# A macaron layer on one core: VectorE's stream steps beside the first FFN go behind the product of each FFN step, and the streams get more steps between engines

## The chip, the core and the metric

One core of one Trainium2 chip runs the whole layer in one launch. A core has five engines that work side by side, each through its own queue in order: TensorE (PE, with its weight loads as PEld), VectorE (DVE), ScalarE (ACT), GpSimd (POOL), and SyncE (SP), which here only starts DMA transfers. They wait for each other through semaphores. The metric is the device time of the core in microseconds, lower is better; for the kernel before it is the median of three runs.

## The reference

The layer takes x of shape (4, 1024, 128): 4096 tokens of width 128. It adds half of a routed FFN, then an attention block, then half of the same FFN again. Cut to what matters:

```python
x = x + 0.5 * ffn(layernorm(x))      # 8 experts, all computed; weights by a router
x = x + attn(layernorm(x))           # 16 heads of 64, low-rank q/k/v through 64 latents, rope
x = x + 0.5 * ffn(layernorm(x))

def ffn(x):
    inh = sigmoid(x @ Wr / temperature)
    in_zone = (inh >= LOWER) & (inh <= 0.5)
    w = exp(-|inh - 1/e| / 0.1) * in_zone
    fb = exp(-|inh - 1/e| / 0.3), kept for its two largest of 8, normed to sum 1
    w = where(sum(w) < 1e-8, fb, w);  w = w / max(sum(w), 1e-8)
    h = silu(x @ Wg[e]) * (x @ Wu[e])          # for each expert e
    return sum over e of w[e] * (h @ Wd[e])

def attn(x):                          # its result already holds x as the residual
    h = layernorm(x) * ln_scale + ln_bias
    cq, ckv = h @ w_down_q.T, h @ w_down_kv.T
    q, k = rope(cq @ w_up_q.T), rope(ckv @ w_up_k.T);  v = ckv @ w_up_v.T
    return softmax(q @ k.T / 8) @ v @ w_out.T + x
```

## The kernel before

**Main loops.** The tokens lie in X, in SBUF, as eight blocks of 512. The program has three stretches. The first FFN (`ffn`) runs 64 steps n, eight blocks by eight experts. A step is six matmuls of 512 columns (L411: gate and up, each in three parts), Silu on ScalarE (L413), the product of Silu and up on VectorE (L419, the "product"), and four matmuls down (L382) for a step three earlier; then a gather adds the result, weighted by the router, to X: by VectorE (L390) for a few experts, else by ScalarE into `dtmp` (L394) and POOL (L395). Gate and up of step n take two of three PSUM banks in turn, so that the gate of step n+2 writes the bank that the product of step n has read: if a product is late, TensorE waits two steps on. The attention runs 128 groups g of four slots: scores (L723), exponentials (L727), running sums on POOL (L739), values (L746), maxima for a later group (L697, L698), and every other group the denominators (`den`, L758) and the output (L779, L790). The second FFN (`ffn2`) runs 64 steps again (L490, L493, L503, L504, L498, L445).

**Streams.** What prepares later work is written as Python generators, which the loops advance a step at a time, so that their instructions are interleaved by hand in each engine's queue. `ffn_pre` prepares two blocks for an FFN: statistics on VectorE (`stats`, L216 and L219), inverse root on POOL (`power`, L223 to L226), norm on ScalarE (`norm`, L235), transposes on PE (L264), a split into two parts on VectorE (L266, L267), router matmuls (L277, L278), then `route`, some ten short VectorE steps with a few of ScalarE and POOL. `attn_pre` prepares a batch for attention: the same twice over, then latents (L555, L561, L562) that go to DRAM (the store at L564) and come back for `rope`. `rope` makes rotated q and k of 512 tokens (matmuls L605, four VectorE products L592, POOL L613, L615, L624, ScalarE L620, two stores to DRAM). In a generator, work k of the first half-block and work k minus a lag of the second are emitted in the same step, so the numbers k set the distance between an instruction and what needs it.

**Who advances them.** Beside the first FFN, `bg1` is called at four points of a step: before gate and up, before down, before the product, behind the product. It gives each stream credit (`bg`): stream 0 (`ffn_pre`) RATE1/4 = 0.6 steps a point, stream 2 (weights, `attn_pre(0)`, nine ropes) RATE2/4 = 0.575. In the attention `step` is called three times a group and takes what the stream's next kind allows (OTHER, VECTOR or PE); VECTOR steps are taken in every group while `hurry` holds (g below 16 or in the last 24), else in even groups. Beside the second FFN `bg2` advances the last `ffn_pre` one step an FFN step from n = 17, two from n = 22. All transposes and small matmuls of the streams beside the first FFN use one PSUM bank (`aux`), so each waits until the one before has been read.

Of the kernel before, what the change touches and what calls it, by code (L numbers as in the profile page):

```python
# [13 lines left out]
ALU = mybir.AluOpType  # L14
# [20 lines left out]
NROPE = 9  # L35
ACTS = (4, 6, 7)
WLAG, GS, GD = 4, 17, 22
RATE0, RATE1, RATE2, RATE3 = 1.55, 2.4, 2.3, 1.4


class Kernel:
# [176 lines left out]
            for i in range(4):  # L218
                nc.vector.bn_aggr(mv[:, i, :], st[:, i, :])  # L219

    def power(self, mv, rstd):
        nc = self.nc
        nc.gpsimd.tensor_scalar(rstd[:, :, 1], mv[:, :, 1], EPS, None, ALU.add)  # L223
        nc.gpsimd.tensor_tensor(rstd[:, :, 0], rstd[:, :, 1], self.neghalf[:, :4], ALU.pow)
        nc.gpsimd.tensor_tensor(rstd[:, :, 1], mv[:, :, 0], rstd[:, :, 0], ALU.mult)
        nc.gpsimd.tensor_scalar(rstd[:, :, 1], rstd[:, :, 1], -1.0, None, ALU.mult)  # L226

    def norm(self, out, src, mv, rstd, half, vector=False):

# [8 lines left out]
    def ffn_pre(self, P, blks, xs, w_out, done=None, rows=None):  # L238
        nc = self.nc
        X = self.X  # L240
        n = len(blks)
        mv = P.tile([128, TPB, 2], F32, name="mvf")
        rstd = P.tile([128, TPB, 2], F32, name="rstdf")
        z = P.tile([128, TPB, E], F32, name="z")
        st = {}

        def stage(k, h, blk):
            t0 = 4 * blk
            hs = slice(4 * h, 4 * h + 4)
            src = [X[:, t0 + i, :] for i in range(4)]  # L250
            if k == 0:
                st["st", h] = self.small.tile([128, 4, 6], F32, name="st")
            if k in (0, 1):
                self.stats(st["st", h], src, mv[:, hs], k)
            elif k == 3:
                self.power(mv[:, hs], rstd[:, hs])
            elif k in (5, 6):
                if k == 5:
                    st["y", h] = P.tile([128, 4, 128], F32, name="yf", tag="f0")
                self.norm(st["y", h], src, mv[:, hs], rstd[:, hs], k - 5, blk == 0 and done is None)  # L260
            elif k == 8:
                ps = self.aux()
                for i in range(4):
                    nc.tensor.transpose(ps[:, i * 128:(i + 1) * 128], st["y", h][:, i, :], self.ident)  # L264
                x2 = st["x", h] = xs(blk)
                nc.vector.tensor_copy(x2[:, 0, :], ps)  # L266
                nc.vector.tensor_tensor(x2[:, 1, :], ps, self.f(x2[:, 0, :]), ALU.subtract)  # L267
                self.ready.add(blk)
            elif k == 12:
                x2 = st["x", h]  # L270
                if done:
                    done(blk, x2)
                pz = self.aux()
                for i in range(4):
                    c = slice(i * 128, (i + 1) * 128)
                    for hl in range(2):
                        nc.tensor.matmul(pz[:, i * 16:(i + 1) * 16], x2[:, hl, c], self.wr[:, hl, :], start=hl == 0, stop=hl == 1)  # L277
                nc.vector.tensor_reduce(z[:, hs, :], pz[:, 0:64].rearrange("p (t k e) -> p t e k", t=4, k=2), AX.X, ALU.add)  # L278

        lag = 9 if blks[0] == 0 and done is None else 5  # L280
        for k in range(14 + lag * (n - 1)):
            yield self.kind([k - lag * h for h in range(n)], (0, 1), (8, 12))
            for h, blk in enumerate(blks):
                stage(k - lag * h, h, blk)
        yield from self.route(P, 4 * n, z, w_out)
        if rows is not None:
            yield from self.weight_rows(P, rows)
        self.routed.update(blks)

    def route(self, P, T, z, w_out):  # L290

        nc = self.nc
        v, act, pool = nc.vector, nc.scalar.activation, nc.gpsimd
# [20 lines left out]
        pool.tensor_scalar(ge, inh, LOWER, None, ALU.is_ge)  # L314
        pool.tensor_scalar(le, inh, UPPER, None, ALU.is_le)
        pool.tensor_tensor(ge, ge, le, ALU.mult)
        yield VECTOR
        v.reciprocal(dx, dx)
        yield OTHER
# [2 lines left out]

        below = new("below", [E, E], "f1")
        pool.tensor_tensor(below, fb.unsqueeze(3).to_broadcast(sh4), self.tri.unsqueeze(1).to_broadcast(sh4), ALU.mult)
        yield VECTOR
        v.tensor_tensor(w, w, ge, ALU.mult)
        yield from more
# [183 lines left out]
    def attn_pre(self, b):  # L511
# [9 lines left out]
        def stage(k, h):  # L521
            t0 = b * TPB + 4 * h
            q = slice(4 * h, 4 * h + 4)
            src = [X[:, t0 + i, :] for i in range(4)]
            y = st.get(("y", h))
            if k in (0, 7):
                st["st", h] = self.small.tile([128, 4, 6], F32, name="st")
            if k in (0, 1):
                assert 2 * b + h in self.done
                self.stats(st["st", h], src, mv[:, q], k)  # L530
            elif k == 2:
                self.power(mv[:, q], rstd[:, q])
            elif k in (4, 5):
                if k == 4:
                    y = st["y", h] = P.tile([128, 4, 128], F32, name="ya", tag=f"{tag}1")
                self.norm(y, src, mv[:, q], rstd[:, q], k - 4)
            elif k in (7, 8):
                self.stats(st["st", h], [y[:, i, :] for i in range(4)], mv2[:, q], k - 7)
            elif k == 9:
                self.power(mv2[:, q], rstd2[:, q])  # L540
                nc.gpsimd.tensor_tensor(X[:, t0:t0 + 4, :], X[:, t0:t0 + 4, :], y, ALU.add)
            elif k in (11, 12):
                if k == 11:
                    st["y2", h] = P.tile([128, 4, 128], F32, name="ya2", tag=f"{tag}2")
                self.norm(st["y2", h], [y[:, i, :] for i in range(4)], mv2[:, q], rstd2[:, q], k - 11)
            elif k == 14:
# [5 lines left out]
            elif k in (17, 20):  # L552
                i = (k - 17) // 3
# [9 lines left out]
            elif k in (18, 21):  # L563
                self.dma(out=self.c_scr[b][h][:, (k - 18) // 3], in_=st["C", h])  # L564
                self.latents.add((b, (k - 18) // 3, h))
            elif k == 24:
                assert b < 2 or self.slot > 128 * (b - 1)
                pt = self.aux()
                for i in range(4):
                    nc.tensor.transpose(pt[:, i * 64:(i + 1) * 64], st["ckT", h][:, i * 128:(i + 1) * 128], self.ident[0:64, 0:64])  # L570
                nc.vector.tensor_copy(self.ckn[b % 2][:, 4 * h:4 * h + 4, :], pt[:, 0:256].rearrange("p (t l) -> p t l", t=4))

        for k in range(25 + 9):

            held = (lambda: k == 24 and b >= 2 and self.slot < 128 * (b - 1) + 4)
            yield lambda: NEVER if held() else self.kind([k - 9 * h for h in range(2)], (0, 1, 7, 8), (14, 17, 20, 24))
            for h in range(2):
                stage(k - 9 * h, h)

    def rope(self, n, stage):  # L580

# [212 lines left out]
    def run(self):  # L794
# [6 lines left out]

        credit = [0.0] * len(streams)

        def bg(k, rate):

            credit[k] += rate
            while credit[k] > 0.999:
                credit[k] -= 1
                while streams[k] and next(streams[k][0], self) is self:
                    streams[k].pop(0)  # L810

        ring = ExitStack()
# [4 lines left out]
        with ExitStack() as ctx:  # L817
# [20 lines left out]
            def bg1(n, point):  # L838
# [98 lines left out]
        for g in range(NGRP + 1):  # L937
# [135 lines left out]
```

## Time and profile before

| what | value |
|---|---|
| median of three runs | 1696.05 us (1694.99 to 1701.25) |
| the profiled execution: its time / its span | 1694.49 us / 1692.7 us |
| first Silu of the first FFN / of the second | 11.50 us / 1538.14 us |
| PE busy, 34.0 to 228.6 us (steps 5 to 63 of the first FFN) | 176.66 us of 194.6 |
| POOL busy, 250 to 1325 us (groups with ropes) | 1044.25 us of 1075 |
| PE busy, 1467 to 1535 us (last groups, no stream but a tail) | 66.62 us of 68 |
| PE busy, 1630 to 1683 us (second FFN, no stream) | 53.00 us of 53 |

The span is what the profiler's records cover; the device time of the same execution is 1.79 us longer. A row of instructions gives the line, the engine, the operation, out<-in with their shapes, and how often; in a list of waits the last three numbers are the total in us, how often, and the longest. PEclk is the share of TensorE's clock that was granted: at 0.5 the same matmuls take twice as long.

### The profile page before, as it was taken

Reading aid. Unit: us, or ns where it says so; the run is one execution under the profiler, and the core shown is the slowest. Engines: PE = TensorE matmul, PEld = TensorE weight load, DVE = VectorE, ACT = ScalarE, POOL = GpSimd, SP = SyncE. Lnnn points to the kernel's source line nnn. Section 1 sums busy time; section 2 is a strip of 40 time slices with the busy share of each in tenths; the row PEclk is TensorE's granted clock in tenths of the full one; section 3 lists DMA queues with packets and bytes.
Section 4 is the critical chain, followed back from the end, with each engine's and each line's share of the span. In section 5 each row is a group of like instructions: output and inputs, shape, how many; then the busy total and the mean of one; then the engine's idle time right before and its main releaser. Section 6 shows DMA issues by size and latency. Waiting matters only on the chain.

```text
span 1692.7 us, 31828 instructions
## 1 busy us (share of the span) xinstructions
PE 1630.9 (96%) x11428; PEld 1057.3 (62%) x11428; DVE 1317.3 (78%) x2672; ACT 924.8 (55%) x1916; POOL 1483.7 (88%) x899
## 2 busy tenths in 40 slices
PE   6898989999999999999999999999999999999998
PEld 5776765665656566666556666565566556556777
DVE  5677667887878888788788888887888876846887
ACT  4576656555555555555555555555555554555554
POOL 5558789999999999999999999999999986786666
PEclk9999999999999999999999999999999999999999
DMA  6023556554444555554455555555556533034543
GB/s 209 1 75 126 174 159 157 159 151 127 126 126 139 138 151 148 147 132 127 125 151 137 140 138 140 126 139 138 144 135 151 121 81 76 2 90 125 148 127 100
DMA packets 241422, 216.04 MB, mean 128 GB/s; under 512 B 156784, under 2 KB 169712, under 8 KB 240624
## 3 DMA queue, kind: packets, MB, share of 16 engines
q1 hardware_dynamic: 241264, 214.01, 46.9%
q8 instruction: 90, 1.47, 0.4%
q14 instruction: 68, 0.56, 0.1%
HBM read 129.93 MB, written 84.02 MB: 126 GB/s over the span
## 4 chain that ended last, share of the span: by engine, by line
PE 59%; POOL 7%; DVE 4%; issue 2%; ACT 2%; SPq 1%; DMA 1%; DVEq 0%; POOLq 0%; ACTq 0%
PE psc L746 19%; PE ps_s L723 18%; POOL acc L739 5%; PE ps_a L697 5%; PE ps_s L490 3%; PE ps_s L758 3%; PE psx L723 2%; PE psx L445 2%; PE psx L779 1%; ACT p L727 1%; PE psx L605 1%; PE ps_s L779 1%; PE psc L490 1%; DVE m L698 1%; PE ps_s L605 1%
## 5 line engine op out<-in xcount | busy, mean ns | idle before, releaser
L698 DVE TENSOR_REDUCE m<-ps_a 128x1 f32<-128x512 f32 x1024 | 684.7, 689 | 224.6 <-PE ps_a L697 193.1
L739 POOL TENSOR_TENSOR acc<-acc,p 128x1024 f32<-128x1024 f32 x320 | 762.3, 2382 | 31.7 <-ACT p L727 12.3
L727 ACT ACTIVATE p<-ps_s 128x512 f32<-128x512 f32 x896 | 479.5, 601 | 302.2 <-PE ps_s L723 289.4
L723 PE MATMUL ps_s<-QT,KT 64*128 64x512 f32 x2688 | 551.9, 399 | 8.9 <-ACT p L727 8.1
L746 PE MATMUL psc<-p,ckn 128*64 128x512 f32 x2048 | 467.7, 598 | 0.0
L723 PEld LDWEIGHTS ps_s<-QT,KT 64*128 64x128 f32 x2688 | 351.4, 185 | 147.9 <-issue 86.0
L697 PE MATMUL ps_a<-KT,QT 64*128 64x512 f32 x1024 | 419.2, 420 | 7.8 <-DVE m L698 6.6
L746 PEld LDWEIGHTS psc<-p,ckn 128*64 128x64 f32 x2048 | 135.6, 136 | 256.7 <-issue 250.8
L723 PE MATMUL ps_s<-maxr,one_row 64*128 64x512 f32 x896 | 240.0, 393 | 0.0
L697 PEld LDWEIGHTS ps_a<-KT,QT 64*128 64x128 f32 x1024 | 185.3, 185 | 40.0 <-DVE m L698 16.7
L739 POOL TENSOR_TENSOR acc<-p 128x1024 f32<-128x1024 f32 x64 | 152.8, 2388 | 29.5 <-ACT p L727 29.3
L624 POOL TENSOR_TENSOR eo<-eo,hi_r 128x1024 fp32r<-128x1024 f32 x64 | 153.4, 2397 | 0.0
L748 ACT COPY osb<-psc 128x512 f32<-128x512 f32 x64 | 37.6, 587 | 194.5 <-PE psc L746 194.5
L723 PEld LDWEIGHTS ps_s<-maxr,one_row 64*128 64x128 f32 x896 | 124.3, 186 | 14.1
L395 POOL TENSOR_TENSOR X<-X,dtmp 128x512 f32<-128x512 f32 x54 | 69.6, 1288 | 57.7 <-ACT dtmp L394 57.2
L723 PE MATMUL psx<-QT,KT 64*128 64x512 f32 x384 | 111.9, 396 | 0.0
L498 POOL TENSOR_TENSOR p<-eo,p 128x512 fp32r<-128x512 f32 x42 | 63.5, 1519 | 38.3 <-ACT p L497 37.5
L613 POOL TENSOR_TENSOR eo<-rt,rt 128x512 f32<-128x512 f32 x64 | 82.7, 1292 | 2.0 <-DVE rt L592 2.0
L615 POOL TENSOR_TENSOR eo<-rt,rt 128x512 f32<-128x512 f32 x64 | 83.0, 1297 | 0.0
L790 DVE SCALAR_TENSOR_TENSOR X<-ps_s,rT,X 128x128 f32<-128x128 f32 x252 | 70.9, 344 | 13.9 <-PE ps_s L779 7.2
L727 ACT ACTIVATE p<-psx 128x512 f32<-128x512 f32 x128 | 76.8, 600 | 5.2 <-PE psx L723 1.1
L620 ACT CAST hi_r<-eo 128x512 fp32r<-128x512 f32 x128 | 73.9, 624 | 10.1 <-POOL eo L613 6.2
(197 smaller groups left out, 2467.7 us busy)
## 6 DMA issues: line engine op xcount, KB each, us to landing
C_l<-cs SPq DMA_DIRECT2D x64, 512.0 KB
QT<-qs SPq DMA_DIRECT2D x256, 128.0 KB
KT<-ks SPq DMA_DIRECT2D x256, 128.0 KB
qs<-hi_r SPq DMA_DIRECT2D x32, 512.0 KB
qs<-eo SPq DMA_DIRECT2D x32, 512.0 KB
ks<-hi_r SPq DMA_DIRECT2D x32, 512.0 KB
ks<-eo SPq DMA_DIRECT2D x32, 512.0 KB
wb<-wt SPq DMA_DIRECT2D x64, 256.0 KB
```

Of the source, the lines that this page charges most:

```text
L395: nc.gpsimd.tensor_tensor(X[:, t:t + 4, :], X[:, t:t + 4, :], tmp, ALU.add)
L613: nc.gpsimd.tensor_tensor(w["eo"][:, 0, :], w[0, 0], w[1, 1], ALU.subtract)
L615: nc.gpsimd.tensor_tensor(w["eo"][:, 1, :], w[0, 1], w[1, 0], ALU.add)
L620: nc.scalar.copy(w["hi"][:, k, :], w["eo"][:, k, :])
L624: nc.gpsimd.tensor_tensor(w["eo"].bitcast(F32R), w["eo"], self.f(w["hi"]), ALU.subtract)
L697: nc.tensor.matmul(self.psA[hh], self.QT[P % 3][r, 0, q0:q0 + 128], self.KT[P % 3][r, 0, kk * 512:kk * 512 + 512], start=True, stop=True)
L698: nc.vector.tensor_reduce(m[0][:, hh, qb, kk:kk + 1], self.psA[hh], AX.X, ALU.max)
L723: nc.tensor.matmul(ps, w, x, start=k == 0, stop=k == 3)
L727: nc.scalar.activation(self.p_of[s][:, hh, :], ps, AF.Exp, scale=0.125)
L739: nc.gpsimd.tensor_tensor(acc, self.p_of[s - 1] if c == 1 else acc, self.p_of[s], ALU.add)
L746: nc.tensor.matmul(self.psC[64 * hh:64 * hh + 64, :], self.ckn[b % 2][:, c, :], self.p_of[s][:, hh, :], start=c == 0, stop=c == 7)
L790: nc.vector.scalar_tensor_tensor(x, po[hh][:, i * 128:(i + 1) * 128], rT[:, 4 * hh + i:4 * hh + i + 1], x, ALU.mult, ALU.add)
```

## The change

It does five things. (1) `bg` knows the kind of the stream's next step; beside the first FFN a VECTOR step of stream 0 is taken only at the point behind the product, one for each FFN step (two if three or more steps of credit have gathered). The rates go up. (2) In `ffn_pre` the norm comes four steps behind `power` instead of two, the transposes three behind the norm's second half instead of two, and so on: 17 instead of 14 numbers; in `attn_pre` 29 instead of 25, with the lag of the second half 11 instead of 9. (3) `route` has three more OTHER steps, one before the reciprocal and two before the first product, except for the first two blocks. (4) For block 0, whose norm is on VectorE, `power` leaves out its two last POOL instructions. (5) `hurry` holds for the last 30 groups instead of 24. The diff, with the renumbering of `attn_pre` cut to its pattern:

```diff
-RATE0, RATE1, RATE2, RATE3 = 1.55, 2.4, 2.3, 1.4
+RATE0, RATE1, RATE2, RATE3 = 1.75, 2.6, 2.5, 1.4
...
-    def power(self, mv, rstd):
+    def power(self, mv, rstd, bias=True):
...
-        nc.gpsimd.tensor_tensor(rstd[:, :, 1], mv[:, :, 0], rstd[:, :, 0], ALU.mult)
-        nc.gpsimd.tensor_scalar(rstd[:, :, 1], rstd[:, :, 1], -1.0, None, ALU.mult)
+        if bias:
+            nc.gpsimd.tensor_tensor(rstd[:, :, 1], mv[:, :, 0], rstd[:, :, 0], ALU.mult)
+            nc.gpsimd.tensor_scalar(rstd[:, :, 1], rstd[:, :, 1], -1.0, None, ALU.mult)
...
             elif k == 3:
-                self.power(mv[:, hs], rstd[:, hs])
-            elif k in (5, 6):
+                self.power(mv[:, hs], rstd[:, hs], blk > 0 or done is not None)
+            elif k in (7, 8):
...
-            elif k == 8:
+            elif k == 11:
                 ps = self.aux()
...
-            elif k == 12:
+            elif k == 15:
                 x2 = st["x", h]
...
-        lag = 9 if blks[0] == 0 and done is None else 5
-        for k in range(14 + lag * (n - 1)):
-            yield self.kind([k - lag * h for h in range(n)], (0, 1), (8, 12))
+        lag = 12 if blks[0] == 0 and done is None else 5
+        for k in range(17 + lag * (n - 1)):
+            yield self.kind([k - lag * h for h in range(n)], (0, 1), (11, 15))
...
-        yield from self.route(P, 4 * n, z, w_out)
+        yield from self.route(P, 4 * n, z, w_out, blks[0] > 0 or done is not None)
...
+        if late:
+            yield OTHER
         yield VECTOR
         v.reciprocal(dx, dx)
...
+        if late:
+            yield OTHER
+            yield OTHER
         yield VECTOR
         v.tensor_tensor(w, w, ge, ALU.mult)
...
-            elif k in (4, 5):
+            elif k in (6, 7):
...
-            elif k in (11, 12):
+            elif k in (15, 16):
...
-        for k in range(25 + 9):
+        for k in range(29 + 11):
...
-        def bg(k, rate):
+        kinds = {}
+
+        def bg(k, rate, vector=NSLOT):
             credit[k] += rate
             while credit[k] > 0.999:
+                gen = streams[k][0] if streams[k] else None
+                if kinds.get(gen) == VECTOR:
+                    if not vector:
+                        break
+                    vector -= 1
                 credit[k] -= 1
-                while streams[k] and next(streams[k][0], self) is self:
+                while streams[k]:
+                    v = next(streams[k][0], self)
+                    if v is not self:
+                        kinds[streams[k][0]] = v() if callable(v) else v
+                        break
                     streams[k].pop(0)
...
-            for n in range(12):
+            for n in range(15):
                 next(first)
-                if n in (5, 6):
+                if n in (7, 8):
                     next(wgen)
...
-                    bg(0, RATE1 / 4)
+                    bg(0, RATE1 / 4, (1 if credit[0] < 3 else 2) if point == 3 else 0)
...
-            hurry = g < 16 or g >= NGRP - 24
+            hurry = g < 16 or g >= NGRP - 30
```

More of the change, by code (lines that the diff above doesn't have):

```diff
@@ L255, in stage @@
             elif k == 3:
-                self.power(mv[:, hs], rstd[:, hs])
-            elif k in (5, 6):
-                if k == 5:
+                self.power(mv[:, hs], rstd[:, hs], blk > 0 or done is not None)
+            elif k in (7, 8):
+                if k == 7:
                     st["y", h] = P.tile([128, 4, 128], F32, name="yf", tag="f0")
-                self.norm(st["y", h], src, mv[:, hs], rstd[:, hs], k - 5, blk == 0 and done is None)
-            elif k == 8:
+                self.norm(st["y", h], src, mv[:, hs], rstd[:, hs], k - 7, blk == 0 and done is None)
+            elif k == 11:
                 ps = self.aux()
@@ L288, in ffn_pre, with route @@
         self.routed.update(blks)
-    def route(self, P, T, z, w_out):
+    def route(self, P, T, z, w_out, late):
         nc = self.nc
@@ L525, in stage @@
             y = st.get(("y", h))
-            if k in (0, 7):
+            if k in (0, 9):
                 st["st", h] = self.small.tile([128, 4, 6], F32, name="st")
@@ L532, in stage @@
                 self.power(mv[:, q], rstd[:, q])
-            elif k in (4, 5):
-                if k == 4:
+            elif k in (6, 7):
+                if k == 6:
                     y = st["y", h] = P.tile([128, 4, 128], F32, name="ya", tag=f"{tag}1")
[L536 to L539, printed above, removed]
+                self.norm(y, src, mv[:, q], rstd[:, q], k - 6)
+            elif k in (9, 10):
+                self.stats(st["st", h], [y[:, i, :] for i in range(4)], mv2[:, q], k - 9)
+            elif k == 11:
                 self.power(mv2[:, q], rstd2[:, q])
                 nc.gpsimd.tensor_tensor(X[:, t0:t0 + 4, :], X[:, t0:t0 + 4, :], y, ALU.add)
-            elif k in (11, 12):
-                if k == 11:
+            elif k in (15, 16):
+                if k == 15:
                     st["y2", h] = P.tile([128, 4, 128], F32, name="ya2", tag=f"{tag}2")
-                self.norm(st["y2", h], [y[:, i, :] for i in range(4)], mv2[:, q], rstd2[:, q], k - 11)
-            elif k == 14:
+                self.norm(st["y2", h], [y[:, i, :] for i in range(4)], mv2[:, q], rstd2[:, q], k - 15)
+            elif k == 18:
                 ps = self.aux()
@@ L551, in stage @@
                 nc.scalar.activation(st["hT", h], ps, AF.Identity, bias=self.lnsb[:, 1:2], scale=self.lnsb[:, 0:1])
-            elif k in (17, 20):
-                i = (k - 17) // 3
+            elif k in (21, 24):
+                i = (k - 21) // 3
                 pc = self.aux()
@@ L562, in stage @@
                 nc.vector.tensor_tensor(C[:, 1, :], pc, self.f(C[:, 0, :]), ALU.subtract)
[L563 to L566, printed above, removed]
+            elif k in (22, 25):
+                self.dma(out=self.c_scr[b][h][:, (k - 22) // 3], in_=st["C", h])
+                self.latents.add((b, (k - 22) // 3, h))
+            elif k == 28:
                 assert b < 2 or self.slot > 128 * (b - 1)
@@ L571, in stage @@
                 nc.vector.tensor_copy(self.ckn[b % 2][:, 4 * h:4 * h + 4, :], pt[:, 0:256].rearrange("p (t l) -> p t l", t=4))
-        for k in range(25 + 9):
-            held = (lambda: k == 24 and b >= 2 and self.slot < 128 * (b - 1) + 4)
-            yield lambda: NEVER if held() else self.kind([k - 9 * h for h in range(2)], (0, 1, 7, 8), (14, 17, 20, 24))
+        for k in range(29 + 11):
+            held = (lambda: k == 28 and b >= 2 and self.slot < 128 * (b - 1) + 4)
+            yield lambda: NEVER if held() else self.kind([k - 11 * h for h in range(2)], (0, 1, 9, 10), (18, 21, 24, 28))
             for h in range(2):
-                stage(k - 9 * h, h)
+                stage(k - 11 * h, h)
     def rope(self, n, stage):
```

## The prediction

> **What bounds the kernel now.** First the page: the engines, then slices of 42.3 us.
>
> ```profile
> PE 1630.9 (96%) x11428; PEld 1057.3 (62%) x11428; DVE 1317.3 (78%) x2672; ACT 924.8 (55%) x1916; POOL 1483.7 (88%) x899
> PE   6898989999999999999999999999999999999998
> POOL 5558789999999999999999999999999986786666
> ```
>
> PE bounds the whole, but from slice 7 to 31 POOL is as full, so stretches must be read apart. Beside the first FFN I take the windows in which PE is not full, and within them the granted clock.
>
> ```profile
> 70.00:103.40 33.40, 28.27 (x154) 23.51 (x152) 19.02 (x73) 22.25 (x64) 20.57 (x33) 0.90 0.04 17
> 132.40:177.20 44.80, 38.55 (x222) 30.69 (x221) 33.22 (x60) 26.62 (x75) 38.78 (x31) 0.96 0.53 169
> ...
> 79.20:86.10 6.90, 6.11 (x19) 5.15 (x20) 5.41 (x22) 3.42 (x10) 5.86 (x10) 0.51 0.01 4
> 154.30:157.80 3.50, 3.50 (x13) 1.99 (x12) 3.26 (x12) 1.10 (x2) 1.38 (x2) 0.51 0.43 147
> ```
>
> Columns: window, length, busy PE, PEld, DVE, ACT, POOL, clock. Zone 1 loses 33.40 - 28.27 = 5.1 us idle, and its matmuls from 79.2 to 86.1 ran at half clock, 6.11 / 2 = 3.1: 8.2 us. Zone 2 loses 6.25 + 3.50 / 2 = 8.0. The windows between (34 to 70, 103.4 to 132.4, 177.2 to 228.6) have 2.1, 1.5 and 3.0 us of idle PE: 6.6. The timeline says what PE waited for, first in zone 1, then in zone 2.
>
> ```profile
> 77.17 0.88 ACT L235 ACTIVATE yf<-X,rstdf 128x128 f32<-128x128 f32 x2 [1.63 <-POOL rstdf L226]
> 77.72 0.71 PE L264 MATMUL ps_s<-ident,yf 128*128 128x128 f32 x2 [2.11 <-ACT yf L235]
> ```
>
> ```profile
> 148.32 1.98 DVE L330 TENSOR_SCALAR ne<-ws 128x8 f32<-128x8 f32 x1
> 150.22 0.16 DVE L331 TENSOR_SCALAR some<-ws 128x8 f32<-128x8 f32 x1
> 150.29 1.75 DVE L334 TENSOR_TENSOR g<-ex,below 128x512 f32<-128x512 f32 x1
> 152.08 0.69 DVE L336 TENSOR_REDUCE le<-g 128x64 f32<-128x512 f32 x1
> 152.68 0.68 DVE L419 TENSOR_TENSOR p<-p,ps_s 128x512 f32<-128x512 f32 x1
> ```
>
> In zone 1 a norm stands in ACT's queue before POOL has its inverse root, and the transposes in PE's queue before the norm: step 18 (Silu to Silu, 71.83 to 78.95) takes 7.12 us, a quiet one 2.25. In zone 2 the route's short steps stand ahead of the product; PE's next gate, which needs that bank, waited 3.6 us and started at 153.41.
>
> The attention I read by its waits between 250 and 1325 us (ACT's between 250 and 1350).
>
> ```profile
> ACT ya L235 <- POOL rstd L226: 25.7, 6, 6.2
> ...
> POOL acc L739 <- ACT p L727: 8.8, 17, 0.9
> ```
>
> ACT stood 25.7 us behind late inverse roots; but POOL itself waited for anything only 8.8 us in 1075. It is asked for all of its time, so it decides what such a stall is worth.
>
> **The change, part by part.**
>
> *The norms further from their roots (zone 1).* `power` takes 2.0 us on POOL (75.18 to 77.13: 0.23, 1.04, 0.20, 0.24 and gaps), the norm 0.88 for a half. In the built order, block 4's root and norm were emitted in one FFN step (18); now the root stands in step 19 and the norm in 21, two steps or 4.5 us apart, which covers 2.0 and one add to X of 1.3 (L395). Not all goes: step 21 now holds three roots and `attn_pre`'s add to X, 3 x 2.0 + 1.3 = 7.3 us of POOL, and the norm that needs the second of them stands 1.5 steps (3.4 us) behind, after 1.3 + 2 x 2.0 = 5.3: about 1.9 us on ACT. ACT's queue before Silu 23 holds four norm halves and a gather, 4 x 0.88 + 1.14 = 4.7 us in a step of 2.25 to 3.1. I leave 2.7 of the 8.2 us and take a gain of 5.5; the ends are 0 (the burst costs what the old one did) and 8.2. The later L395 is covered by three `dtmp` buffers, three steps or 6.8 us; with that gone ACT's gathers wait as in the row of 4.4 us (L394 behind wts).
>
> *The steps behind the product (zone 2).* Nothing is taken away; it is spread. By start to start in the timeline: reciprocal 0.95, L326 to L331 3.2, L334 and L336 2.4, L339 to L350 3.1, L352 to L357 1.1, four rope products 2.4, a gather 1.1, a product 0.6. Before, the queue ahead of products 38 to 41 held 3.4, 5.6, 3.1, 3.5 plus four products: 18.0 us in four steps; PE's own work there is 4 x 2.25 and two ropes of 0.96, 10.9; the steps took 16.7 (142.93 to 159.66). Now it stands ahead of 42 to 47 as 3.4, 0, 6.7, 2.4, 3.1, 3.5 plus six products: 22.7 us, against 6 x 2.25 + 3 x 0.96 = 16.4 for PE. The surplus is 6.3 us where it was 7.1; the old one showed as 5.8 and with it 1.1 of wait behind the gather L390, which is now inside the sum. So some 5.2 us stay of 8.0: gain 2.8. Ends: 0 (the ropes, which the gate does not hold, fall on the same steps) and 8.0.
>
> In 3.2 + 2.4 us of L326 to L336 alone, L330 took 1.98 us where L331, the same form, took 0.16, and POOL's L624 ran meanwhile; the sums above hold this. The Trainium skill ("SBUF — State Buffer", section "SBUF: two separate sides") calls the ports that VectorE and GpSimd share "an exclusive lock, not a bandwidth split". By that rule spreading does not shorten these steps, since POOL is as busy at 42 to 47. The page speaks against the change here; were the steps free of POOL (L330 1.8, L334 1.1 shorter) the surplus would be 3.4 instead of 6.3.
>
> *Rest of the first FFN.* The two POOL instructions left out (0.20, 0.24) stood off the path: the first norm, on DVE, waited for L224 alone. The route of blocks 0 and 1 keeps its place, and so its stall of 2.8 us (L411 behind L419, step 4). The weights of blocks 2 and 3 are now ready one step before their first gather, in the same queue. Ropes come one step later, and their DMAs (C_l, qs, ks) with them; load(0) stays at step 46 behind the fourth rope's store. I take 0; ends -3 and +3 (the 3.0 of the last window doubled or gone).
>
> *Attention.* Every norm there is now over one group (9.7 us) behind its root, so the six waits of ACT go. Their price on PE:
>
> ```profile
> 501.98 0.88 ACT L235 ACTIVATE ya<-X,rstd 128x128 f32<-128x128 f32 x2 [6.21 <-POOL rstd L226]
> ...
> 503.39 0.79 PE L723 MATMUL ps_s<-QT,KT 64*128 64x512 f32 x1 [3.29 <-ACT p L727]
> ```
>
> With half clock from 502.5 to 509.3 (5.91 us busy, half of it lost) that pair of groups took 26.93 us between two L748 instead of 19.45, and the pair at 797.3 took 25.41. But POOL worked through both. Its instructions stay, so the stretch can't become shorter than its 8.8 us of waits allow. I take 4; ends 0 and 8.8. The DMAs that move: `attn_pre`'s stores of latents, past loads of QT, KT and the maxima; batch 1's second half now is stored in group 14 and fetched at the end of 15, a group for two transfers (C_l took 5.8 us in the chain of waits). If late, PE waits as in "PE psx L605 <- DMA C_l<-cs", 1.3 us. The stores of x2 move likewise and are read long after. `hurry` shifts route steps from even groups to all between 98 and 104: no count changes, 0.
>
> *Second FFN.* From 1583 to 1630 PE idles 1.15 + 0.61 + 2.64 = 4.4 us, and 3.09 / 2 = 1.5 is lost at half clock (1622 to 1625.5): 5.9. Norms waited 2.85 and 1.20 us for roots and L326 1.89 us for POOL; the new distances remove these, while DVE's pile (L334 again 1.78) stays. I take 2; ends -4 and 5.9. The lower one: the store of the last weights (at 1634.65) now stands behind three more loads `wb`, two steps before the first load that reads it, and four more before its use; late by two steps it costs 4.
>
> **Sum:** 5.5 + 2.8 + 0 + 4 + 2 = 14.3 us. The profiled execution took 1694.49 (span 1692.70 and 1.79 around it), so 1680.2; it lies 1.56 below the median of the runs, so 1681.8, said as 1682. Each term at its better and worse third gives its own range, 1673 to 1690.
>
> **Rivals.**
> *A: the gain stays in zone 1.* The gate holds stream 0 alone; the ropes' four products (2.4 us) still stand ahead of products, zone 2 keeps its 8 us, and POOL gives the attention nothing. For it: POOL's 8.8 us, and surplus 6.3 against 7.1. Against: six long ACT waits with half clock behind them. 1696.05 - 5.5 + 1 = 1691.5.
> *B, slower: POOL's lag reaches the denominators.* The root at 499.99 was emitted at about 492: POOL ran 8 us late. The stall let it catch up (POOL idle 1.5 us in the next pair). Without stalls the lag stays, and from one group (9.7 us) on `den` (L758 behind L739) and the rope cast (L620 behind L613) wait on every pair. Price: a wait of 1 us, then half clock for 3.4 (1.7 lost); in ten of the 26 pairs of 500 to 1000 us 27 us, less 8.3 of the FFN: 1696 + 19 = 1715. For it: POOL without slack. Against: L758 waited for POOL once, 0.6 us, and the same work passed before.
> *C: all of it.* The upper ends of zones, attention and second FFN, 8.2 + 8.0 + 8.8 + 5.9 = 31, less a fifth: 1671.
>
> **How the numbers follow.** Forecast 0.52, A 0.24, B 0.13, C 0.11. This kernel's measurement tells 0.5% (8.5 us) from no change: faster is below 1687.5, slower above 1704.5. Of the forecast 0.49 lies below 1687.5 and 0.03 between; with C, faster is 0.60. A gives 0.22 within and 0.02 slower; B is slower: within 0.25, slower 0.15. The range leaves a tenth out at each side: from inside C, 1666, to between A and B, 1700.
>
> **What would show it.** Right: in the changed kernel no norm waits over 1 us for a root in the attention, both long pairs are near 20 us; half clock near 79 us is gone; Silu to Silu, steps 18 to 26 sum to 6 us less; steps 41 to 48 still hold waits of L411 for L419. POOL from the first attention pair on has less than 8 us of waits. Wrong: the last Silu of the first FFN is not 5 to 12 us earlier; or L758 and L620 wait for POOL again and again; or wb's loads wait for the weight store.

## The result and the profile after

| | kernel before | changed kernel |
|---|---|---|
| median of 12 runs each, side by side | 1697.27 us | 1701.65 us |
| profiled execution, span | 1692.7 us | 1699.4 us |
| last Silu of the first FFN | 225.67 us | 231.09 us |
| table load ahead of the first Silu of the second FFN | 1538.14 us | 1545.97 us |

The ratio is 1.0023, with a 95% interval of 1.0013 to 1.0034: slower by 0.1 to 0.3%. That is less than the 0.5% that the prediction took as its bound for "slower", but on the other side of the forecast and 1.65 us above the upper end of its range. The time given above as the second FFN's first Silu, 1538.14, is that of the load of its activation table; the Silu itself comes 1.29 us later, in both kernels. The page of the changed kernel, engines and slices, shows the same work in more time:

```profile
PE 1626.0 (96%) x11428; PEld 1054.5 (62%) x11428; DVE 1327.7 (78%) x2672; ACT 927.5 (55%) x1916; POOL 1483.3 (87%) x897
PE   6988889999999999999999999999999999999998
POOL 5548689999999999999999999999998987786766
```

VectorE has the same 2672 instructions and is busy 10.4 us longer. Cut at the same events (Silus of the first FFN by number, output copies L748/L754 of the attention, one for each pair of groups), the two profiled executions differ so; the column "forecast" is the prediction's sum:

| stretch | before, us | after, difference | forecast |
|---|---|---|---|
| start to Silu 18 | 71.83 | -2.07 | 0 |
| Silu 18 to 27 (zone 1) | 36.75 | +1.36 | -5.5 |
| Silu 27 to 38 | 34.35 | +0.88 | 0 |
| Silu 38 to 51 (zone 2) | 44.58 | +4.66 | -2.8 |
| Silu 51 to first output copy | 76.38 | +0.33 | 0 |
| output copies 0 to 48 (48 pairs of groups) | 981.62 | -1.49 | -4 |
| copy 48 to the second FFN | 292.64 | +4.17 | in the 4 |
| second FFN and tail | 154.55 | -1.15 | -2 |

The windows of zones 1 and 2, first Silu 17 to 25, then Silu 38 to 51 of the changed kernel (columns as in the prediction):

```profile
67.49:98.55 31.06, 23.64 (x134) 19.82 (x133) 21.12 (x78) 19.40 (x54) 18.71 (x28) 0.89 0.00 1
143.09:192.33 49.24, 38.95 (x219) 30.99 (x219) 36.69 (x61) 26.03 (x73) 39.23 (x32) 0.97 0.60 189
```

The clock dip of zone 1 is still there (0.89). In zone 2 of the kernel before, VectorE was busy 32.63 us with the same 61 instructions. The timeline of zone 1 in the changed kernel, steps 22 and 23:

```profile
81.34 0.59 ACT L419 ACTIVATE p<-ps_s 128x512 f32<-128x512 f32 x1
...
85.38 0.88 ACT L236 ACTIVATE yf<-X,rstdf 128x128 f32<-128x128 f32 x2 [3.44 <-POOL rstdf L227]
...
89.47 0.59 ACT L419 ACTIVATE p<-ps_s 128x512 f32<-128x512 f32 x1
...
90.09 0.69 DVE L425 TENSOR_TENSOR p<-p,ps_s 128x512 f32<-128x512 f32 x1 [5.95 <-ACT p L419]
...
91.06 1.08 PE L555 MATMUL ps_s<-ident,ya 128*128 128x128 f32 x4 [6.07 <-DVE z L279]
```

The wait has moved, not gone: a norm stands 3.44 us in ACT's queue before its root, the next Silu behind it comes 8.13 us after the one before, and PE stands 6.07 us before the transposes of `attn_pre` (L555). The timeline of zone 2, steps 45 to 47:

```profile
170.46 2.39 POOL L630 TENSOR_TENSOR eo<-eo,hi_r 128x1024 fp32r<-128x1024 f32 x1
170.49 2.90 DVE L340 TENSOR_TENSOR g<-ex,below 128x512 f32<-128x512 f32 x1
...
178.31 2.40 POOL L630 TENSOR_TENSOR eo<-eo,hi_r 128x1024 fp32r<-128x1024 f32 x1
178.43 2.35 DVE L356 TENSOR_TENSOR ex<-ex,fr 128x64 f32<-128x64 f32 x1
180.71 0.67 DVE L425 TENSOR_TENSOR p<-p,ps_s 128x512 f32<-128x512 f32 x1
...
181.44 0.96 PE L417 MATMUL ps_s<-xs,wg 128*128 128x512 f32 x3 [3.03 <-DVE p L425]
```

Each of these two long steps of the route starts just after one of POOL's rope subtractions and ends about with it or half a us later; the product stands behind it. In the attention, the waits of PE between 264 and 1245 us before, then those of PE and of ACT in the changed kernel:

```profile
PE ps_s L723 <- ACT p L727: 7.2, 3, 3.3
...
PE ps_a L697 <- DVE m L698: 0.8, 2, 0.6
```

```profile
PE ps_a L703 <- DVE m L704: 6.1, 6, 2.0
PE ps_s L764 <- POOL acc L745: 4.6, 4, 1.6
...
ACT hi_r L626 <- POOL eo L619: 7.5, 8, 2.1
ACT hi_r L626 <- POOL eo L621: 7.1, 14, 0.6
```

No norm waits for a root any more. In their place denominators (L764) and rope casts (L626) wait for POOL, and PE's largest waits are now those of the maxima matmuls (L703), whose bank VectorE has not read yet: 6.1 us in six where it was 0.8 in two.

### The profile page after: what moved, and what is told of

The parts are those of the page before. It is cut to its first block, busy times and chain, and to the rows that moved or that the text cites. A ratio compares the mean times of both kernels' runs of the same rounds, so it can differ in the third digit from the quotient of the medians.

```text
span 1699.4 us, 31824 instructions
## 1 busy us (share of the span) xinstructions
PE 1626.0 (96%) x11428; PEld 1054.5 (62%) x11428; DVE 1327.7 (78%) x2672; ACT 927.5 (55%) x1916; POOL 1483.3 (87%) x897
## 4 chain that ended last, share of the span: by engine, by line
PE 67%; POOL 10%; DVE 7%; ACT 4%; issue 4%; SPq 2%; DMA 1%; POOLq 0%; DVEq 0%; ACTq 0%
PE psc L752 20%; PE ps_s L729 20%; POOL acc L745 6%; PE ps_a L703 6%; PE ps_s L764 3%; PE psx L729 3%; PE ps_s L417 2%; PE ps_s L496 2%; PE psx L785 2%; PE psx L451 2%; DMA dT<-d 1%; ACT p L733 1%; PE psx L611 1%; SPq L50 1%; DVE m L704 1%
## 5 line engine op out<-in xcount | busy, mean ns | idle before, releaser
L745 POOL TENSOR_TENSOR acc<-acc,p 128x1024 f32<-128x1024 f32 x320 | 762.8, 2384 | 31.1 <-ACT p L733 11.6
L703 PE MATMUL ps_a<-KT,QT 64*128 64x512 f32 x1024 | 420.2, 421 | 14.7 <-DVE m L704 13.8
L703 PEld LDWEIGHTS ps_a<-KT,QT 64*128 64x128 f32 x1024 | 184.9, 184 | 49.0 <-DVE m L704 25.2
L754 ACT COPY osb<-psc 128x512 f32<-128x512 f32 x64 | 37.6, 587 | 197.0 <-PE psc L752 197.0
L626 ACT CAST hi_r<-eo 128x512 fp32r<-128x512 f32 x128 | 75.6, 625 | 24.3 <-POOL eo L619 13.8
```

Of the source, the lines that this page charges most:

```text
L626: nc.scalar.copy(w["hi"][:, k, :], w["eo"][:, k, :])
L703: nc.tensor.matmul(self.psA[hh], self.QT[P % 3][r, 0, q0:q0 + 128], self.KT[P % 3][r, 0, kk * 512:kk * 512 + 512], start=True, stop=True)
L745: nc.gpsimd.tensor_tensor(acc, self.p_of[s - 1] if c == 1 else acc, self.p_of[s], ALU.add)
```

## The experiments

Each ratio is to the kernel before, run beside it, from 4 to 12 runs of each kernel. The stretches come from one profiled execution each; runs of one program spread over up to 12 us, and the same first FFN differed by up to 2.7 us between two profiles (the changed kernel and hurry25). The profiled execution of the kernel before (1694.49) lies about 3 us below the medians of its runs beside these kernels (1697 to 1699), so the differences to it are some 3 us too large in sum. That of nogate_nolate24 (1698.16) lies 6.5 us above the median of its own runs. The differences are in us: from the start to Silu 63, over the 48 pairs, from copy 48 to the second FFN, and over the second FFN.

| kernel | ratio (95% interval) | Silu 63 | 48 pairs | copy 48 on | FFN 2 |
|---|---|---|---|---|---|
| changed kernel | 1.0023 (1.0013-1.0034) | +5.4 | -1.5 | +4.2 | -1.0 |
| gate_only | 1.0110 (1.0087-1.0133) | +16.5 | +1.6 | +0.3 | -0.1 |
| space_rates | 1.0001 (0.9989-1.0012) | +0.2 | +2.6 | +5.6 | -1.0 |
| attn_old | 1.0098 (1.0078-1.0118) | +10.9 | +5.1 | +4.3 | -2.0 |
| hurry25 | 0.9997 (0.9982-1.0013) | +8.1 | -0.2 | +0.6 | -2.1 |
| nogate_h25 | 0.9986 (0.9977-0.9995) | +0.7 | -1.4 | +0.2 | -1.0 |
| nogate_nolate | 0.9977 (0.9963-0.9990) | +4.7 | -1.5 | +0.4 | -3.1 |
| gate_route | 1.0032 (1.0020-1.0044) | +4.5 | -1.0 | +5.9 | -1.0 |
| before_h30 | 1.0048 (1.0030-1.0066) | +0.9 | +3.7 | +5.9 | +0.6 |
| attn_new | 1.0036 (1.0023-1.0050) | +6.9 | +0.8 | +1.5 | -0.2 |
| nogate_nolate24 | 0.9957 (0.9941-0.9973) | +3.4 | +3.1 | +1.8 | -3.1 |
| both_again | 0.9973 (0.9961-0.9984) | +3.7 | -0.2 | +1.6 | -3.1 |
| first13 | 1.0014 (1.0004-1.0025) | +8.2 | -1.0 | +0.5 | -2.1 |
| no_rank | 1.0016 (1.0006-1.0027) | +3.7 | -0.3 | +4.1 | -1.0 |
| pool_light | 0.9881 (0.9864-0.9898) | +1.0 | -11.5 | -2.6 | +0.8 |
| ffn_new | 1.0011 (1.0000-1.0023) | +4.3 | +4.7 | +2.1 | -3.1 |
| late1 | 0.9967 (0.9955-0.9980) | -0.3 | +3.9 | +0.9 | -3.2 |

**The gate.** gate_only adds it, with the new rates, to the kernel before; space_rates takes the gate out of the changed one.

```diff
-                    bg(0, RATE1 / 4)
+                    bg(0, RATE1 / 4, (1 if credit[0] < 3 else 2) if point == 3 else 0)
```

> The kernel before with the gate in bg and the new rates alone; old distances in the streams, hurry 24. Theory (the gate makes the loss in zone 2, because a VECTOR step still stands ahead of the next product and now in every step): the last Silu of the first FFN 3 to 6 us later than before (225.67), and the whole 1700 to 1703 us. Rival (the gate is neutral; the longer streams push the route of the last blocks onto the ropes): last Silu within 1.5 us of before, the whole 1696 to 1698.

> The changed kernel without the gate: the new distances, the later route steps, the new rates and hurry 30 stay. Theory (the gate makes the loss in zone 2): last Silu of the first FFN 3 to 6 us earlier than in the changed kernel (231.09), the whole 1696 to 1699. Rival (distances and late route steps make it): last Silu still near 231, the whole 1700 to 1703.

space_rates did as the theory said (1697.74, last Silu at 225.8). The gate costs: 1.0110 where distances are old (the new rates in it were not tried alone), and with new ones 1.0023 against 1.0001. gate_only lost three times what the theory said, and elsewhere: step 17 took 7.43 us (2.27 before) and step 29 10.45 (2.59). Its timeline in step 29:

```profile
121.28 0.23 POOL L223 TENSOR_SCALAR rstdf<-mvf 128x4 f32<-128x4 f32 x1 [7.20 <-DVE mvf L219]
...
123.27 1.65 ACT L235 ACTIVATE yf<-X,rstdf 128x128 f32<-128x128 f32 x4 [3.85 <-POOL rstdf L226]
...
123.82 1.63 PE L264 MATMUL ps_s<-ident,yf 128*128 128x128 f32 x4 [3.85 <-ACT yf L235]
```

Root, norm and transposes follow one another without a gap, and PE stands behind them. The order in which the generators are advanced shows why. While a VECTOR step waits for its point the stream saves credit, and behind the product it spends it at once: for block 6 the root leaves in step 28, and both norm halves and the transposes in one burst behind the product of step 29. In the kernel before, these stand 0.75 to 2 steps behind the root.

gate_route keeps the gate for the route alone:

```diff
-            yield self.kind([k - lag * h for h in range(n)], (0, 1), (11, 15))
+            yield self.kind([k - lag * h for h in range(n)], () if done is None else (0, 1), (11, 15))
```

> The changed kernel with its gate for the route's VECTOR steps alone; the statistics of blocks 2 to 7 pass at any point, as without the gate. hurry 30. Theory (the harm of the gate is that steps held behind the statistics leave in one burst, so that root, norm and transposes come closer): steps 34 and 35 back from 6.59 + 1.48 to some 6.1 in sum, and 3 to 5 us less at the last Silu than in the changed kernel (231.09): 226 to 228; the whole 1697 to 1699. Rival (the harm is the route's steps ahead of the products): last Silu 229.5 to 231.5, the whole 1700 to 1703.

Last Silu at 230.19 and 1701.49 us: the rival. With the new distances the burst is not what costs; holding back the route is. (Without the gate the same first FFN ended at 225.4 to 226.4 in three profiles.) no_rank leaves two VectorE steps out of that route, for blocks 6 and 7:

```diff
-        v.tensor_tensor(g, fb.unsqueeze(2).to_broadcast(sh4), below, ALU.is_gt)
+        if not skip:
+            v.tensor_tensor(g, fb.unsqueeze(2).to_broadcast(sh4), below, ALU.is_gt)
```

> The changed kernel, in which the first FFN's route of blocks 6 and 7 leaves out two VectorE steps, the comparison g (L340, 2.90 us in the changed kernel) and its sum le (L342, 0.69); their weights are then not the reference's. Theory (the route's steps ahead of the products set the loss in zone 2): Silu 38 to Silu 51, 49.2 us in the changed kernel, 3 us shorter or more, last Silu at 226 to 228. Rival (ropes and POOL set it, the steps only fill the gaps): less than 1.5 us shorter, last Silu 229.5 to 231.

Silu 38 to 51 took 46.2 us, 3.0 less, as the theory had it, but the last Silu came at 229.4, 0.1 below the rival's range, since Silu 38 had come 1.3 us later. The route's steps do set part of zone 2; two of them are not all of it.

**Hurry.** hurry25 changes one number of the changed kernel, before_h30 the same number of the kernel before.

```diff
-            hurry = g < 16 or g >= NGRP - 30
+            hurry = g < 16 or g >= NGRP - 25
```

> The changed kernel with hurry over the last 25 groups in place of 30. Theory (VECTOR steps in every group from 98 to 104 make the row maxima late): the three pairs of groups between 1249 and 1316 us (22.86, 22.09, 22.22) come back to 19.5 to 20.5, later pairs give some of it back, the whole 3 to 5 us below the changed kernel. Rival (the steps only move): within 1 us of it.

> The kernel before with hurry over 30 groups in place of 24, nothing else. Theory (VECTOR steps in every group from 98 on make the row maxima late by themselves): some pairs of groups between 1245 and 1325 us of 22 us and more, the whole 3 to 6 us above the kernel before. Rival (only with the longer attn_pre): within 1.5 us of the kernel before.

Both as the theory said: 1697.61 against 1701.65, and 1706.32 against 1697.08 (9.2 us, where 3 to 6 were foreseen; 5.9 of it from copy 48 on). The three pairs of groups from output copy 48 on, sum over the windows, of the kernel before and then of the changed one:

```profile
sum 59.60, PE 58.84 PEld 36.50 DVE 50.99 ACT 31.48 POOL 58.51; mean PE 19.61 PEld 12.17 DVE 17.00 ACT 10.49 POOL 19.50
```

```profile
sum 67.10, PE 61.12 PEld 37.79 DVE 61.68 ACT 31.89 POOL 59.46; mean PE 20.37 PEld 12.60 DVE 20.56 ACT 10.63 POOL 19.82
```

VectorE has gone from 51.0 of 59.6 us to 61.7 of 67.1, that is 92% of the time, and the row maxima come late: until they have read their bank, PE's next maxima matmul (L703, L697 before) stands, and the scores behind it. The waits of PE between 1245 and 1325 us, before and after:

```profile
PE ps_a L697 <- DVE m L698: 1.0, 2, 0.8
```

```profile
PE ps_a L703 <- DVE m L704: 5.3, 5, 1.5
```

**Distances.** attn_old takes the old attn_pre into the changed kernel, attn_new the new one into the kernel before; ffn_new does so with ffn_pre.

```diff
-            elif k in (4, 5):
+            elif k in (6, 7):
...
-        for k in range(25 + 9):
+        for k in range(29 + 11):
```

> The changed kernel with the old distances in attn_pre alone (all four batches). Theory (in the attention POOL sets the time, so that the stalls of ACT cost little): the long pairs of groups come back (two of 25 us or more), the waits of the denominators for POOL go, and the whole stays within 3 us of the changed kernel, 1699 to 1705. Rival (the new distances earned what these two pairs lost, 7.5 and 4.1 us): 1709 to 1714.

> The kernel before with the new distances in attn_pre alone (and stream 2's rate 2.5, that it ends in time); no gate, old ffn_pre, hurry 24. Theory (in the attention the new distances earn what the prediction said, some 3 to 4 us, POOL keeping the rest): no pair of 25 us among the groups 25 and 55, denominators wait for POOL between 800 and 910 us; from the first output copy to the second FFN 2 to 4.5 us shorter than before (1274.3), the whole 1692 to 1696. Rival (POOL keeps all): within 1 us, the whole 1696 to 1699.

> The kernel before with the new distances in ffn_pre alone (17 numbers, lag 12 for the first pair, no bias for block 0, rates 1.75, 2.6, 2.3); old attn_pre, no gate, no later route steps, hurry 24. Theory (attn_pre's distances earn nothing net, so that the gain of nogate_nolate24 is that of ffn_pre's): 1690 to 1694, ratio 0.995 to 0.9975. Rival (it needs attn_pre's too): 1696 to 1700.

attn_old: 1715.01, more than the rival's upper end, but 5.5 us of it lie in the first FFN, where attn_pre(0) runs too. attn_new: the long pairs went, but copy 0 to the second FFN took 1276.5 us, 2.3 more, and the first FFN 6.9 more: theory and rival were both wrong. ffn_new: 1700.48, the rival. Either set alone is slower than none (for ffn_new the interval begins at 1.0000). first13 starts attn_pre(0) two steps earlier:

```diff
-                if n == 15:
+                if n == 13:
                     streams[2].append(self.attn_first())
```

> nogate_h25 with attn_pre(0) put into stream 2 at step 13 in place of 15, so that its norms no longer fall on the steps of those of blocks 4 and 5. Theory (zone 1 is lost in bursts of roots and norms from both streams): steps 18 to 29 sum to 3 us less or better than in nogate_h25 (40.44), the whole 1690 to 1692. Rival (the same work of the streams stands ahead of some other Silu): within 1.5 us of it, the whole 1693 to 1696.

Silu 18 to 29 took 44.34 us, not 37.4, and the whole 1701.28: theory and rival were both wrong. It looks as if the bursts only met other work; which, was not traced.

**POOL in the attention.** pool_light leaves out one of POOL's six additions for each pair of groups:

```diff
-        elif c < 8 - DIRECT:
+        elif c < 8 - DIRECT and c != 5:
```

> The kernel before, in which POOL leaves out one of its six additions for each pair of groups (L739 for the sixth slot of eight, 64 of 384, some 2.4 us each; the denominators then lack that slot). Theory (POOL sets the time of the attention, and PE alone would need some 19.45 us a pair): the 48 pairs from the first output copy on, 981.6 us before, go to 935 to 950 (48 x 19.45 = 933.6), no norm waits over 1 us for its root, and the whole falls to 1650 to 1665. Rival (the extra time of the pairs comes of the ropes' own work on PE and of DVE): 48 pairs at 970 or more, the whole 1680 or more.

The 48 pairs took 970.1 us and the whole 1679.44: within a us of the rival's figures. The window 250 to 1325 us, and the waits of POOL and of ACT there:

```profile
250.00:1325.00 1075.00, 1067.48 (x8087) 652.13 (x8087) 898.73 (x1792) 591.49 (x1154) 929.67 (x507) 1.00 0.54 141
```

```profile
POOL acc L739 <- ACT p L727: 123.0, 60, 4.0
...
ACT ya L235 <- POOL rstd L226: 2.7, 4, 1.0
```

POOL now stands 123 us and the pairs of 20 to 22 us stay; PE is busy in 1067.48 of the 1075 us, so they are filled by PE's own work. Only the two pairs of 26.93 and 25.41 us shrank much, to 20.50 each, 11.3 us in sum; the other 46 differ by 0.2 in sum. So POOL did not set the pace; its lateness cost the stalls, 11.3 us.

**Versions without gate and with a short hurry.** nogate_h25 is the changed kernel without the gate and with hurry 25. nogate_nolate also leaves out the later route steps in the first FFN; nogate_nolate24 (run again as both_again) leaves them out everywhere, with hurry 24; late1 has them in the first FFN alone, with hurry 24.

```diff
-        yield from self.route(P, 4 * n, z, w_out, blks[0] > 0 or done is not None)
+        yield from self.route(P, 4 * n, z, w_out, blks[0] > 0 and done is None and rows is None)
```

> The changed kernel without the gate and with hurry over 25 groups; new distances, late route steps and new rates stay. Theory (gate and hurry cost each by itself, some 4 and 4.5 us by the runs space_rates and hurry25 against the changed kernel): 1692 to 1694, ratio to the kernel before 0.996 to 0.998. Rival (both runs removed the same loss, POOL's work sets the end of the attention): 1697 to 1699.

> As nogate_h25, but in the first FFN without the three later OTHER steps in route. Theory (they push the last route onto the ropes of steps 44 to 48): last Silu of the first FFN 2 to 5 us earlier than in space_rates (225.8), the whole 1688 to 1691. Rival (the ropes are there either way, and the route's wait for POOL comes back): last Silu within 1.5 us of it or later, the whole 1692 to 1695.

> The changed kernel with its new distances and rates, but no gate, no later route steps anywhere, and the old hurry of 24. Theory (what is left of the change is its distances, and they are worth some 4 us): 1692 to 1695, ratio 0.997 to 0.9985. Rival (each of the groups with hurry costs over 1 us, as 30 against 24 did in before_h30): 1690 to 1692.

> The changed kernel with both sets of new distances, no gate, hurry 24, and the later route steps in the first FFN alone. Theory (each part's stretch adds up: the later steps earn some 3 us in the first FFN, where the last Silu came 0.1 and 0.7 us after that of the kernel before with them and 3.4 and 4.7 us without, and cost some 2 us in the second FFN, 1.0 gained with them and 3.1 without): last Silu at 225 to 227, second FFN 2.5 to 3.5 us shorter than before (144.89), the whole 1688 to 1691, ratio 0.9935 to 0.9955. Rival (what one stretch gains the next gives back): 1692 to 1696.

> nogate_nolate24 once more, beside late1, since its profiled execution (1698.16) lay far above the median of its runs (1691.71): where does its gain lie? Theory (in the attention, where the stalls behind POOL fall differently from one execution to the next): median 1691 to 1694; its profile shows the first FFN 3 to 5 us longer than before as then, and the attention 1 to 4 us shorter. Rival (in the first FFN): last Silu near 226.

nogate_h25: 1694.50, nearer the theory than the rival: gate and hurry cost each by itself, the one up to Silu 63, the other from copy 48 on. nogate_nolate: 1693.51 and the last Silu at 230.4, the rival in both: the later route steps help the first FFN by some 4 us and hurt the second by 1 to 2. nogate_nolate24: 1691.71, the rival's end; run again 1693.73. late1: 1691.17, last Silu 225.4 and second FFN 3.2 shorter as foreseen, the whole between the two cases, since its 48 pairs took 3.9 us more. nogate_nolate, nogate_nolate24 and late1 are faster than the kernel before by 0.1 to 0.6%, nogate_h25 by 0.05 to 0.23%, and so all four are faster than the changed one; which of them is best the intervals don't tell. both_again met the theory in time and in the first FFN (3.7 us longer), but not in the attention: from Silu 63 to the second FFN it took 0.2 us more than before, not 1 to 4 less.

## Why the prediction was wrong

Two parts made the kernel slower, the gate and the longer hurry, and each was shown by taking it out or putting it in. They are not the whole miss: without both (nogate_h25) the median is 2.6 us below that of the kernel before, where 14.3 were forecast. The rest is in the terms one by one.

**Zone 1 (-5.5, measured +1.4).** The step that failed is "I leave 2.7 of the 8.2 us". The place was named rightly: three roots in one step, the second needed 1.5 steps later. But the wait was 3.44 us, not 1.9, and behind it stood norm halves and a gather, so that step 22 took 8.13 us, 5.9 over a quiet one; PE idle, it then ran at a clock of 0.59 from 86.2 to 94.5 us. After Silu 25 the kernel was still 4.8 us ahead, 2.1 of it from before Silu 18; the route's steps on ACT ahead of Silu 27 (step 26: 6.13 us, 2.95 before) took the rest. Without the gate Silu 18 to 38 is 2.4 to 3.2 us shorter than in the kernel before (space_rates, nogate_h25, late1), with it 0.7 to 3.2 longer (gate_route, hurry25, the changed kernel, no_rank). But before_h30 and pool_light, whose first FFN is that of the kernel before, were 1.2 and 1.4 us shorter there too. So the distances were worth a third to a half of the term; the gate took that and more. nogate_nolate, nogate_nolate24 and both_again, which have neither gate nor later route steps in the first FFN, show the term earned and lost again: Silu 18 to 27 took 29.5 us, 7.3 less, at the full clock (1.00), and Silu 27 to 38 gave 5.4 back, 5.0 of it in step 28, where in nogate_nolate PE stood 3.4 us before the transposes of `attn_pre`, behind VectorE's reading of the bank that the streams share. The prediction read the gate only in zone 2.

**Zone 2 (-2.8, measured +4.7).** The step that failed is the sum of 22.7 us, which priced the moved steps at their old durations. They stood ahead of products 42 to 47 as it says, but from start to start L340 and L342 took 3.5 us, not 2.4, and L345 to L356 took 6.1, not 3.1. The whole route of blocks 6 and 7, nineteen instructions, took 10.95 us on VectorE before, 15.16 after (and 13.80 in space_rates); the route of blocks 4 and 5, away from the ropes, 6.60. So the surplus grew by 4.2 where 0.8 less was forecast. L340, which reads two SBUF tiles, took 2.90 us where POOL's subtraction of 2.39 us had begun 0.03 us before it, and 0.69 in the route of blocks 4 and 5. The Trainium skill ("SBUF — State Buffer", section "SBUF: two separate sides") says that of a GpSimd instruction that reads SBUF and a VectorE instruction with two SBUF inputs, the first to start holds a shared port pair for its whole length and the other waits; these rows agree. The prediction took this only as a reason against a gain, not as a price for standing beside other POOL instructions. But this price is not the whole loss. Without the gate zone 2 is 3.2 to 3.9 us longer than in the kernel before (2.0 to 2.9 longer than in before_h30 and pool_light), whether its route took 13.8 us (space_rates, nogate_h25, late1) or, as before, 10.3 to 10.7 (nogate_nolate, nogate_nolate24, both_again). What else lengthens it there was not found.

**Rest of the first FFN (0).** -0.6 in sum up to Silu 63, well inside its ends of -3 and +3.

**Attention (-4, measured +2.4 from Silu 63 to the second FFN).** Two steps failed. "`hurry` ... no count changes, 0" is the larger: counts did not change, but the steps went from groups without rope products (which end at 1354 us) to groups with them, where VectorE was then busy for 92% of the time. Copy 48 to the second FFN took 4.1 to 5.9 us more in all six kernels with 30, and 0.2 to 2.1 in the others but pool_light. The other is that POOL "decides what such a stall is worth": pool_light shows that the stalls were worth their time, 11.3 us for the two. Both long pairs went, to 19.49 and 21.23 us, and no norm waits, as forecast; POOL's waits between 250 and 1325 us are 13.7 us, not under 8. The two pairs gained 11.6 us; that the 48 gained only 1.5 comes for the larger part from a cost that the prediction put at nothing and no rival named. The six pairs in which PE waited for VectorE's row maxima took 10.1 us more in sum than the same pairs before; in one, L340 of a route stood for 2.44 us ahead of the maxima. Rival B's mechanism is there too, but small: beside the second long pair, the three pairs whose denominators waited for POOL took 1.7 us more. POOL's additions and, behind them, the denominators in the changed kernel:

```profile
810.61 4.84 POOL L745 TENSOR_TENSOR acc<-acc,p 128x1024 f32<-128x1024 f32 x2
...
815.50 0.64 PE L764 MATMUL ps_s<-acc,ones 128*32 128x256 f32 x8 [1.58 <-POOL acc L745]
```

Four such waits, 4.6 us, not ten pairs: B was mis-sized (27 us), and did not make the kernel slower by itself. Over all profiles with 25 numbers (five, without pool_light) the 48 pairs average 3.0 us above the kernel before's own, with 29 numbers (twelve) 0.3, so that the term, 4, may hold 2.7; single profiles spread by 5.

**Second FFN (-2, measured -1.0, and -0.2 in the tail).** Right in sign; the later route steps took 1 to 2 of 3.1 (with them the gain is 1.0 to 2.1, without 3.1 to 3.2). The loads of wb were not late: the last twelve steps kept their length.

**Rivals.** A fell, since zone 1 gained nothing, and so did C. The slower outcome came from none of the three but from the gate, forecast as a gain, and from hurry, put at nothing.

**What stays open.** What lengthens zone 2 beside the route, and why VectorE's maxima are late in those six pairs beyond the one route step. Why each set of distances alone is slower and both together faster; the stretches show that what one place gains another often gives back, not which meeting of steps decides. The long pair near group 61 (23.6 to 26.6 us in five profiles with old distances, 21.4 in that of the kernel before) was not traced.

## What to carry to other kernels

A gate on one kind of step is also a delay of all that stands behind it in the same stream, and with credit saved meanwhile it can turn spacing into bursts, as in gate_only: look at what leaves together, not only at what is held. Moving steps at equal counts is not free; price them by what the engine and its port neighbour do at the new place, and check how full the engine is there. An engine that is busy for 97% of a stretch need not set its pace: take a part of its work away and look before costing stalls at nothing.

## What the runs showed of the hardware

The same VectorE instruction took 0.69 or 2.90 us (L340) and 0.22 or 2.14 us (L332, in the routes of blocks 4 and 5 and of 6 and 7), by what POOL ran beside it. The 143 whole routes of all 18 profiles have 2717 VectorE steps; 686 took over 0.25 us more than the shortest of their kind, and when they began POOL was busy with an instruction, every time. Where that instruction was longer than 0.9 us, the excess was, in the median, what was left of it less 0.13 us. No reduction and no reciprocal is among the 686, though 311 reductions and reciprocals began beside a POOL instruction that ran on for over 0.6 us past their own shortest time. With POOL relieved of 64 additions, POOL's busy time fell by 115 us in 1075, and PE's pairs hardly changed but for the two long ones.
